# Selective scans: two of sixteen B products made from transposes, and B loads in two buffers instead of three

## The chip, the cores and the metric

The kernel runs on one core of one Trainium2 chip. The metric is the device time of one execution in microseconds (us). Before the change, three runs gave 34,249.87, 34,252.28 and 34,259.34 us; their median, 34,252.28 us, is what a new time is compared with.

## The reference

The reference is a chain of four residual layers on an image of 256 x 256 positions with 128 channels: attention, a state-space layer with selective scans (layer 1), a Fourier layer and a recurrent filter. Ahead of each stands a group norm. Only layer 1 is touched by the change in its arithmetic. Its core:

```python
xs = jnp.concatenate([x_hwwh, jnp.flip(x_hwwh, axis=-1)], axis=1)   # 4 directions
x_dbl = jnp.einsum('bkdl,kcd->bkcl', xs, x_proj_w)
dts, Bs, Cs = jnp.split(x_dbl, [DT_RANK, DT_RANK + D_STATE], axis=2)  # 8, 16, 16 rows
...
def step(h, inp):
    d_t, x_t, B_t, C_t = inp
    dA = jnp.exp(d_t[..., None] * As)
    h = dA * h + (d_t * x_t)[..., None] * B_t[:, :, None, :]
    y = jnp.einsum('bkdn,bkn->bkd', h, C_t)
    return (h, y)
```

There are 4 directions, 256 inner channels, 16 states and 65,536 positions. For each direction, channel, state n and position t, the scan needs a factor exp(delta · A), an input delta · x · B with B the same for all channels, and its result is multiplied by C, also the same for all channels, and summed over the states.

## The kernel before, in words

The scans are `scan_stream` (from line 562). It walks over 512 chunks: four directions (k = 0 and 1 forward, 2 and 3 backward; 1 and 3 over the transposed image), each with 128 chunks of 512 positions. Channels lie on the partitions, in two halves `dh` of 128; positions lie along the row. States are handled in four groups of G = 4. One chunk is therefore NG = 8 steps, numbered `j` (or `s` in the loop): step j has half j % 2 and states of group j // 2. `g` counts steps over all chunks.

A step has these parts. `b_product` (L763) multiplies four rows of B, spread over all partitions (`l1b_bb`, 128 x 4 x 512), by delta · x (one row of 512 per channel) and gives `l1b_db`. Steps 2, 4 and 6 do this on GpSimd with a copy of delta · x in SBUF (`l1b_dus`, made by ScalarE at L752); the others do it on VectorE with delta · x in PSUM (`l1b_mm` for half 0, `l1b_du` for half 1). `scans` makes each pair of states in turn: ScalarE writes exp(delta · A) for two states into a PSUM tile `l1b_da` (L781, two tiles used in turn), sets the column where the second state begins from the state kept from the last chunk (L785), and VectorE runs one scan over both states, 1,024 columns (L796). After the first pair ScalarE keeps the last column of the step before (`keep_state`, L807). `c_product` (L811, GpSimd) multiplies the four scans by C (`l1b_cc`), and `sums` (L830, TensorE) adds the results into PSUM by products with the identity, two steps later. `y_out` (L839, ScalarE) copies the sum, and every second chunk SP stores two chunks of y (L643).

Beside this, the next chunk is prepared: `dt` (L699) and the two identity products `soft_sum` (L725) make delta through softplus (ScalarE L711 to L719), `delta_copy` (L733) keeps it, `delta_x` (L741, VectorE) multiplies it by x, in step 4 for half 0 (into `l1b_mm`) and in step 7 for half 1 (into `l1b_du`). `xproj` (L667) and `xd_copy` (L679) make the 40 rows of delta's input, B and C two chunks ahead; SP writes B and C to DRAM (L681) and reads them back spread over the partitions with `load_b` (L687) and `load_c` (L693), 1 MB each, four of each per chunk.

The order of all this is written out by hand. `tc.manual_schedule()` makes every engine's queue follow the order of the program text, and all DMAs here go through SP's queue in that order too. `b_order` says which products stand ahead of which step (numbers from 8 on belong to the next chunk: product 8 in step 4, product 10 in step 6); `extras` says what stands after the first and the second scan of a step. Product 9 stands in step 7. `load_b` for group g // 2 + 4 and `load_c` for g // 2 + 3 stand at the end of the odd steps, B first. Tiles come from pools with a fixed number of buffers: B and C loads 3 each, products 5, scans 3, C products 3. An instruction that would overwrite a buffer waits until its readers are done, and so does everything behind it in its queue.

## Time and profile before

| what | value |
|---|---|
| runs (median) | 34,252.28 us |
| the profiled execution's own time | 34,251.71 us |
| its span, first to last instruction | 34,249.9 us |
| busy: TensorE / VectorE / ScalarE / GpSimd | 85% / 91% / 66% / 80% |
| scan stage 3,904 to 29,500 us, busy: TensorE / VectorE / ScalarE / GpSimd | 21,390 / 24,930 / 18,017 / 25,264 us |
| DMA share in the scan stage | 0.54 |
| mean granted TensorE clock | 0.918 |

A line of a group names the source line, the engine, the operation, what it writes and reads, the shape and the count; after the bar stand the busy total in us, the mean of one in ns, and the idle time of the engine just before such instructions with what ended most of it. In a timeline the columns are start and length in us, engine, line and operation. SPq is the DMA queue of SP: there the length is the time to issue a transfer, not to move it. A window's line has the busy time of each engine, then the granted clock, the mean share of the 16 DMA engines and the GB/s that they moved.

### The profile page before, as it was taken

What the parts mean: (1) busy time and instruction counts of PE and PEld (TensorE: products, weight loads), DVE (VectorE), ACT (ScalarE), POOL (GpSimd) and SP (SyncE); (2) the same over time, 40 slices, a digit from 0 to 9 for tenths busy, and PEclk for the clock granted to TensorE, in tenths of its full rate; (3) what the DMA queues carried; (4) which work ended last, traced back from release to release, by engine and by line L of the source; (5) the groups of instructions that cost most, each with busy time, mean ns of one, the idle gap of its engine ahead of it and who ended that gap; (6) DMA issues with size and microseconds to landing.
All of it is one profiled execution on the core that took longest, in us unless ns stands there. A gap on an engine that the chain in (4) does not pass through costs nothing. (4 is left out here: it accounts for less than half of the span.)

```text
span 34249.9 us, 256893 instructions
## 1 busy us (share of the span) xinstructions
PE 29062.3 (85%) x72308; PEld 12164.1 (36%) x72308; DVE 31137.1 (91%) x23801; ACT 22770.2 (66%) x46991; POOL 27433.4 (80%) x6996
## 2 busy tenths in 40 slices
PE   7999888888888888888888888888888888899988
PEld 3554333333333333333333333333333333334444
DVE  6668999999999999999999999999999999863699
ACT  3667777777777777777777777777777777532476
POOL 2446899999999999999999999999999999620000
PEclk8999999999999999999999999999999999999888
DMA  3113455555555555555555555555555555674111
GB/s 142 45 45 121 183 191 190 192 189 192 191 190 191 190 192 189 192 191 190 197 201 200 201 203 201 201 201 200 200 201 203 201 201 201 212 236 148 63 34 33
DMA packets 2076530, 5947.88 MB, mean 174 GB/s; under 512 B 115207, under 2 KB 1379608, under 8 KB 1499222
## 3 DMA queue, kind: packets, MB, share of 16 engines
q1 hardware_dynamic: 1939122, 5860.18, 47.3%
q10 hardware_dynamic: 135972, 71.27, 0.7%
q8 instruction: 570, 9.34, 0.1%
q14 instruction: 866, 7.09, 0.1%
HBM read 5238.41 MB, written 692.58 MB: 173 GB/s over the span
## 5 line engine op out<-in xcount | busy, mean ns | idle before, releaser
L796 DVE TENSOR_TENSOR_SCAN l1b_h<-l1b_da,l1b_state,l1b_db 128x1024 f32<-128x1024 f32 x8192 | 18792.7, 2336 | 596.9 <-ACT l1b_db L785 583.3
L811 POOL TENSOR_TENSOR l1b_hc<-l1b_h,l1b_cc 128x2048 f32<-128x2048 f32 x4096 | 18447.2, 4528 | 329.0 <-DVE l1b_h L796 328.0
L830 PE MATMUL l1b_y<-l1b_hc,ident 128*128 128x512 f32 x32768 | 16062.5, 639 | 1117.0 <-POOL l1b_hc L811 1117.0
L781 ACT ACTIVATE l1b_da<-l1b_dl,l_alog 128x512 f32<-128x512 f32 (+1 forms) x16384 | 11297.5, 690 | 3156.6 <-DVE l1b_h L796 2848.7
L830 PEld LDWEIGHTS l1b_y<-l1b_hc,ident 128*128 128x128 f32 x32768 | 6528.7, 205 | 10690.6 <-issue 8162.7
L763 POOL TENSOR_TENSOR l1b_db<-l1b_bb,l1b_dus 128x2048 f32<-128x2048 f32 x1536 | 6967.3, 4536 | 44.5 <-DMA l1b_bb<-l1b_bc 44.5
L763 DVE TENSOR_TENSOR l1b_db<-l1b_bb,l1b_du 128x2048 f32<-128x2048 f32 x2048 | 4657.8, 2274 | 35.2
L785 ACT ACTIVATE l1b_db<-l1b_state,l1b_db,l1b_af 128x1 f32<-128x1 f32 x8192 | 3045.2, 372 | 0.0
L699 PE MATMUL l1b_mm<-l1b_xd,l_dtw 41*128 41x512 f32 x2048 | 1373.1, 755 | 1712.6 <-ACT l1b_dus L752 1706.8
L725 PE MATMUL l1b_mm<-l1b_tail,ident 128*128 128x512 f32 x2048 | 1292.2, 717 | 1380.9 <-ACT l1b_tail L719 1378.5
L807 ACT COPY l1b_state<-l1b_h 128x4 f32<-128x4 f32 x4095 | 789.6, 193 | 2433.8 <-DVE l1b_h L796 2433.7
L327 POOL TENSOR_TENSOR l0b_e<-l0b_e,l0b_den 128x1024 f32<-128x1024 f32 x512 | 969.0, 1893 | 1373.4 <-DVE l0b_den L326 727.3
L725 PE MATMUL l1b_mm<-l1b_relu,ident 128*128 128x512 f32 x2048 | 1308.8, 728 | 0.0
L699 PEld LDWEIGHTS l1b_mm<-l1b_xd,l_dtw 41*128 41x128 f32 x2048 | 337.8, 206 | 2526.4 <-ACT l1b_dus L752 2129.9
L752 ACT COPY l1b_dus<-l1b_mm 128x512 f32<-128x512 f32 x512 | 299.6, 585 | 1388.5 <-DVE l1b_db L763 1388.1
L763 DVE TENSOR_TENSOR l1b_db<-l1b_bb,l1b_mm 128x2048 f32<-128x2048 f32 x512 | 1171.5, 2288 | 18.2 <-ACT l1b_dus L752 0.7
L303 DVE CUSTOM_DVE_ANT_0 l0b_e<-l0b_sc,l0b_bias 128x256 f32<-128x256 f32 x2048 | 745.4, 420 | 414.5 <-PE l0b_sc L292 411.1
L725 PEld LDWEIGHTS l1b_mm<-l1b_tail,ident 128*128 128x128 f32 x2048 | 376.8, 206 | 2051.5 <-ACT l1b_tail L719 1803.9
L318 ACT ACTIVATE l0b_e<-l0b_e,l0b_top 128x256 f32<-128x256 f32 x2048 | 1012.1, 498 | 0.9 <-DVE l0b_top L303 0.9
L667 PE MATMUL l1b_du<-l1b_xc,l_xproj 128*40 128x512 f32 x2048 | 979.8, 601 | 32.2 <-DMA l1b_xc<-l_xc 31.4
L733 ACT COPY l1b_dl<-l1b_mm 128x512 f32<-128x512 f32 x1024 | 587.4, 574 | 524.2 <-DVE l1b_du L741 517.1
L981 POOL TENSOR_TENSOR l1c_y<-l1c_y,l1c_yt 128x512 f32<-128x512 f32 x256 | 396.3, 1570 | 593.1 <-DMA l1c_y<-l_y 528.4
(275 smaller groups left out, 30094.6 us busy)
## 6 DMA issues: line engine op xcount, KB each, us to landing
l1b_bb<-l1b_bc SPq DMA_DIRECT2D x2048, 1024.0 KB
l1b_cc<-l1b_bc SPq DMA_DIRECT2D x2048, 1024.0 KB
l1b_xc<-l_xc SPq DMA_DIRECT2D x128, 1024.0 KB
l_y<-l1b_yo SPq DMA_DIRECT2D x128, 1024.0 KB
l1b_xc<-l_xct SPq DMA_DIRECT2D x256, 512.0 KB
l_y<-l1b_yo SPq DMA_DIRECT2D x256, 512.0 KB
l_xc<-l1a_o SPq DMA_DIRECT2D x64, 1024.0 KB
l_xct<-l1a_ot SPq DMA_DIRECT2D x16, 4096.0 KB
```

Source lines behind the costliest of these rows:

```text
L318: nc.scalar.activation(e[:, i], e[:, i], AF.Exp, scale=-1.0, bias=top[:, i : i + 1], accum_out=den[:, i : i + 1],)
L327: nc.gpsimd.tensor_tensor(e, e, den[:, :, None].to_broadcast([P, 4, S]), ALU.mult)
L667: nc.tensor.matmul(du1[:40], w["xproj"][:, dh, k, :], in_block(blocks[ch][0], ch, dh), start=dh == 0, stop=dh == 1,)
L699: nc.tensor.matmul(mm, w["dt"][:, chunks[ch][0], dh * P : dh * P + P], xds[ch % 3][0:41], start=True, stop=True,)
L725: nc.tensor.matmul(mm, c.ident, part, start=i == 0, stop=i == 1)
L763: eng.tensor_tensor(db, bbs[g // 2], du[:, None, :].to_broadcast([P, G, CH]), ALU.mult)
L781: nc.scalar.activation(da[:, o + lo : o + hi], dl[:, lo:hi], AF.Exp, scale=w["A"][:, k, dh, n : n + 1])
L785: nc.scalar.activation(first, states[k][:, dh, two : two + 1], AF.Identity, scale=af[:, two : two + 1], bias=first,)
L796: nc.vector.tensor_tensor_scan(h_, a_, d_, states[k][:, dh, one : one + 1], ALU.mult, ALU.add)
L807: nc.scalar.copy(states[k][:, dh, n0 : n0 + G], hs[g][:, :, 0 if k >= 2 else CH - 1])
L811: nc.gpsimd.tensor_tensor(hc, hs[g], ccs[g // 2], ALU.mult)
L830: nc.tensor.matmul(ys[j % 2], c.ident, hc[:, i], start=False, stop=j // 2 * G + i == 15)
```

## The change

States 14 and 15 no longer get their B product from a load of B that is spread over the partitions. For them delta · x is turned: TensorE transposes its four blocks of 128 positions (`du_turn`), so that positions lie on the partitions and channels along the row, and ScalarE copies the result to SBUF (`du_keep`). B's 40 rows are turned in the same way (`b_turn`, `b_keep`), which gives one number per position and state. ScalarE then multiplies with B as the per-partition scale (`b_scale`, eight instructions of 128 x 256 per chunk, both halves in one), and TensorE transposes back (`turn_back`, eight transposes in each of steps 6 and 7) into the PSUM tile of the second pair. In these two half steps the exponentials go to a new SBUF tile `l1b_dat`, and the scan reads its factors there and its inputs in PSUM. The addition to the first column is split: the product with the kept state (`from_state`) first, the addition after the turning. A memset clears one column after step 7.

The products of steps 6 and 7 cover two states (`l1b_dbs`, two buffers); the products of four have four buffers instead of five. B loads have two buffers instead of three, the last load of a chunk is half as large, and each now stands at a step of its own: at the end of steps 0 (group 3), 2 and 3 (groups 0 and 1 of the next chunk) and 7 (its group 2). The C loads stand where they stood. Product 10 moves from step 6 to step 7. `dt` for the next chunk moves behind the scans of step 0. There are two tiles `l1b_xd` instead of three. To make room, the group norms' statistics lie in pools of their own that are closed between layers (this part of the diff is left out).

```diff
-    b_order = {0: (3,), 1: (4,), 2: (5,), 3: (6, 7), 4: (8,), 6: (10,)}
+    T, NT = 14, CH // P
+    b_order = {0: (3,), 1: (4,), 2: (5,), 3: (6, 7), 4: (8,)}
+    turned_at = {(0, 1): (0, 1), (1, 0): (2,), (2, 0): (3,), (3, 0): (4,), (4, 1): (5, 6, 7)}
...
         def load_b(m):
             if m < 4 * N:
-                n0 = m % 4 * G
-                bb = bbs[m] = bcp.tile([P, G, CH], F32, name="l1b_bb")
-                nc.sync.dma_start(bb, bcs[m // 4][n0 : n0 + G][None].to_broadcast([P, G, CH]))
+                n0, n = m % 4 * G, min(G, T - m % 4 * G)
+                bb = bbs[m] = bcp.tile([P, G, CH], F32, name="l1b_bb", bufs=2)
+                nc.sync.dma_start(
+                    bb[:, 0:n], bcs[m // 4][n0 : n0 + n][None].to_broadcast([P, n, CH])
+                )
...
-            db = dbs[g] = wk.tile([P, G, CH], F32, name="l1b_db", bufs=5)
+            n = min(G, T - j // 2 * G)
+            name, bufs = ("l1b_db", 4) if n == G else ("l1b_dbs", 2)
+            db = dbs[g] = wk.tile([P, n, CH], F32, name=name, bufs=bufs)
...
+        def b_turn(ch):
+            for b in range(NT):
+                nc.tensor.transpose(
+                    du1[:, bass.ts(b, 40)], xds[ch % 2][0:40, bass.ts(b, P)], c.ident[0:40, 0:40]
+                )
+        def b_keep(ch):
+            bt = bts[ch] = wk.tile([P, NT, 16 - T], F32, name="l1b_bt")
+            nc.scalar.copy(
+                bt, du1[:, 0 : NT * 40].rearrange("p (b n) -> p b n", b=NT)[:, :, 8 + T : 24]
+            )
+        def du1_copy(ch):
+            dls[ch, "du1"] = wk.tile([P, CH], F32, name="l1b_relu", bufs=1)
+            nc.scalar.copy(dls[ch, "du1"], du1)
+        def du_turn(ch, dh):
+            du = dls.pop((ch, "du1")) if dh else dls[ch, "du"]
+            for b in range(NT):
+                nc.tensor.transpose(mm[:, bass.ts(b, P)], du[:, bass.ts(b, P)], c.ident)
+        def du_keep(ch, dh):
+            nc.scalar.copy(duts[ch][:, :, dh], mm.rearrange("p (b c) -> p b c", b=NT))
+        def b_scale(ch, i):
+            n, b = divmod(i, NT)
+            nc.scalar.activation(
+                turned[ch][:, b, n], duts[ch][:, b], AF.Identity, scale=bts[ch][:, b, n : n + 1]
+            )
+        def turn_back(ch, dh, to):
+            for n in range(16 - T):
+                for b in range(NT):
+                    nc.tensor.transpose(to[:, n, bass.ts(b, P)], turned[ch][:, b, n, dh], c.ident)
...
+                if n0 + 2 * i < T:
+                    dbp = db[:, sl]
+                else:
+                    from_state = wk.tile([P, 1], F32, name="l1b_fs")
...
+                    turn_back(ch, dh, das[i])
+                    dbp, da = da, das_t.rearrange("p g t -> p (g t)")
...
                 if s == 7:
-                    extras[0] = [lambda: delta_x(nxt, 1), lambda: b_product(g + 2)]
-                    extras[1] = [lambda: delta_copy(nxt, 1)]
+                    extras[0] = [
+                        lambda: delta_x(nxt, 1),
+                        lambda: b_product(g + 2),
+                        lambda: b_product(g + 3),
+                    ]
+                    extras[1] = [
+                        lambda: delta_copy(nxt, 1),
+                        lambda: du1_copy(nxt),
+                        lambda: du_turn(nxt, 0),
+                    ]
...
                 c_product(g)
+                if s in (0, 2, 3, 7):
+                    load_b(4 * ch + {0: 3, 2: 4, 3: 5, 7: 6}[s])
                 if s % 2 == 1:
-                    load_b(g // 2 + 4)
                     load_c(g // 2 + 3)
```

Also in the diff: `du_keep(nxt, 0)` and `du_turn(nxt, 1)` at the end of step 7, `du_keep(ch, 1)` after the first scan of step 0, `b_turn(nxt)` at the end of step 4 and `b_keep(nxt)` after the first scan of step 5.

## The prediction, made before the changed kernel was run

> **What bounds it now.** I began with the page's totals and its forty slices.
>
> ```profile
> span 34249.9 us, 256893 instructions
> ...
> PE 29062.3 (85%) x72308; PEld 12164.1 (36%) x72308; DVE 31137.1 (91%) x23801; ACT 22770.2 (66%) x46991; POOL 27433.4 (80%) x6996
> ...
> DVE  6668999999999999999999999999999999863699
> ...
> POOL 2446899999999999999999999999999999620000
> ```
>
> VectorE (DVE) and GpSimd (POOL) are both full from slice 4 to slice 34: the scan stage. It runs from about 3,904 to 29,500 us, and the span (34,249.9 us) stands 1.8 us below its own execution (34,251.7) and 2.4 below the median of the runs (34,252.28), so a sum over the stage can be set on either. Next the costliest groups:
>
> ```profile
> L796 DVE TENSOR_TENSOR_SCAN l1b_h<-l1b_da,l1b_state,l1b_db 128x1024 f32<-128x1024 f32 x8192 | 18792.7, 2336 | 596.9 <-ACT l1b_db L785 583.3
> L811 POOL TENSOR_TENSOR l1b_hc<-l1b_h,l1b_cc 128x2048 f32<-128x2048 f32 x4096 | 18447.2, 4528 | 329.0 <-DVE l1b_h L796 328.0
> ...
> L763 POOL TENSOR_TENSOR l1b_db<-l1b_bb,l1b_dus 128x2048 f32<-128x2048 f32 x1536 | 6967.3, 4536 | 44.5 <-DMA l1b_bb<-l1b_bc 44.5
> L763 DVE TENSOR_TENSOR l1b_db<-l1b_bb,l1b_du 128x2048 f32<-128x2048 f32 x2048 | 4657.8, 2274 | 35.2
> ```
>
> Per chunk of 512 positions that is, on VectorE, 16 scans, 5 B products (L763) and 2 multiplications delta·x (L741, 0.674 us each in the groups of 8,000 to 24,000 us); on GpSimd, 8 C products (L811) and 3 B products. In the timeline L741 of one chunk starts at 12,009.48 and of the next at 12,059.42: a chunk lasts 49.94 us, and 512 of them 25,570. On GpSimd 8 × 4.528 + 3 × 4.536 = 49.8 us. On VectorE the records overlap a little (four scans take 9.07 us, five products 2.2 each), 16 × 2.27 + 5 × 2.2 + 1.35 = 48.7; the rest is two gaps of 0.62 and 0.51 us in steps 5 and 6, where the scan waits for ScalarE (ACT). So two engines bound the stage together, and neither queue has room for a new wait.
>
> The next view is the DMA queue's own timeline, since the change alters the B buffers. L693 loads C, L687 loads B, L643 stores y:
>
> ```profile
> 12035.17 0.32 SPq L693 DMA_DIRECT2D l1b_cc<-l1b_bc  x1
> 12035.58 1.28 SPq L643 DMA_DIRECT2D l_y<-l1b_yo  x2
> 12036.96 3.92 SPq L687 DMA_DIRECT2D l1b_bb<-l1b_bc  x1
> ...
> 12085.11 0.32 SPq L693 DMA_DIRECT2D l1b_cc<-l1b_bc  x1
> 12085.52 0.38 SPq L687 DMA_DIRECT2D l1b_bb<-l1b_bc  x1
> ```
>
> SP issues in order. L693 waits for the C product of step 1 to give back its buffer: 12,106 of the 16,000 us from 8,000 to 24,000, the largest of the queue's waits by far. When that product ends is fixed by GpSimd:
>
> ```profile
> 12021.64 4.52 POOL L811 TENSOR_TENSOR l1b_hc<-l1b_h,l1b_cc 128x2048 f32<-128x2048 f32 x1 [0.66 <-DVE l1b_h L796]
> 12026.13 4.52 POOL L763 TENSOR_TENSOR l1b_db<-l1b_bb,l1b_dus 128x2048 f32<-128x2048 f32 x1
> 12030.62 9.00 POOL L811 TENSOR_TENSOR l1b_hc<-l1b_h,l1b_cc 128x2048 f32<-128x2048 f32 x2
> ```
>
> The C product of step 0 starts when its scans end, the B product of state group 2 follows, then the C product of step 1, without a gap: 3 × 4.49 = 13.5 us, to 12,035.1, where SP issues L693. Last, when VectorE begins the first B product of the next chunk, in step 4:
>
> ```profile
> 12040.03 2.29 DVE L763 TENSOR_TENSOR l1b_db<-l1b_bb,l1b_mm 128x2048 f32<-128x2048 f32 x1
> ...
> 12089.97 2.29 DVE L763 TENSOR_TENSOR l1b_db<-l1b_bb,l1b_mm 128x2048 f32<-128x2048 f32 x1
> ```
>
> 12,040.03 − 12,035.17 = 4.86 us after that issue; 89.97 − 85.11 gives 4.86 again. And when the transfers end, from the windows of 1 us (last two columns: share of the DMA engines, GB/s):
>
> ```profile
> 12045.00:12046.00 1.00, 1.00 (x2) 0.34 (x1) 1.00 (x1) 0.97 (x3) 1.00 (x1) 0.50 0.57 238
> 12046.00:12047.00 1.00, 1.00 (x2) 0.34 (x1) 1.00 (x2) 0.36 (x3) 1.00 (x1) 0.50 0.00 0
> ...
> 12086.00:12087.00 1.00, 1.00 (x4) 0.42 (x3) 1.00 (x1) 0.00 (x0) 1.00 (x1) 1.00 1.02 221
> ...
> 12091.00:12092.00 1.00, 0.00 (x0) 0.00 (x0) 1.00 (x1) 0.00 (x0) 1.00 (x1) 1.00 0.53 221
> ```
>
> After the pair of 12,085.11 (C and B, 1 MB each) the engines move data from 12,086.0 to about 12,091.5: 6.4 us from the issue. In the chunk of 12,035.17, with a y store between, they move until 12,045.9: 10.8 us. The other three directions give 6.1, 6.4 and 6.4, and 10.9 with the store (for the last two, whose next B load comes later, 8.3 for C and y plus 2.6 for one load). The B load of these pairs has a buffer to spare now, so nobody waits for it.
>
> **What the Trainium skill says.** "DMA: Bandwidth & Descriptors", section "Anatomy of one DMA — SWDGE (gpsimd) path", gives a fixed part of about 2.0 us per transfer, most of it after the last byte, and says that a semaphore wait is served by the issuing sequencer before dispatch. Its path is GpSimd's and ours SP's; the trace agrees: first packets 0.9 us after the issue, and at the stage's start, where three loads of 1 MB are issued from 3,897.33 (B, C, B), GpSimd waits for the third:
>
> ```profile
> 3897.33 0.34 SPq L687 DMA_DIRECT2D l1b_bb<-l1b_bc  x1
> ...
> 3907.30 4.50 POOL L763 TENSOR_TENSOR l1b_db<-l1b_bb,l1b_dus 128x2048 f32<-128x2048 f32 x1 [44.51 <-DMA l1b_bb<-l1b_bc]
> ```
>
> The windows there add up to 3 MB at about 3,906.1, so the consumer starts some 1.1 us after the last byte, and the third of three transfers is usable 9.97 us after the first issue. Its section "Bandwidth" has 436 GB/s as the divisor; windows with C and B alone show 377 to 467. "TensorE: Matmul & The Clock Gate", section "Part 4: PE-mode transpose", says that a transpose lands in PSUM and needs a copy, at about 275 ns in a kernel; layer 0's transposes show 280 ns each, 137 ns sustained (561.1 us for 4,096). "Perfetto Trace Analysis", section "Optimization Strategy", reads a gap that repeats on the engine that should be full as a possible lack of buffers; today's two gaps are ScalarE's, so the kernel before does not show that.
>
> **The change part by part,** per chunk, against 49.94 us.
>
> Products of states 12–15, now 2 states instead of 4. VectorE: from 0.674 us for 512 columns and 2.288 for 2,048, 1.05 ns a column, so 1,024 columns are cheaper by 1.08 us. GpSimd: 4.536 to about 2.27, its sum to 47.5: no longer a bound. VectorE gains a memset of one column (0.06). Net −1.02 us, −520 us in all if nothing else waits.
>
> ScalarE adds three copies of 128x512 (0.585), eight scalings of 128x256 (the last layer's 128x256 copies take 0.37 to 0.38), two single columns (0.372) and a small copy (0.2): 5.7 us. It is busy 18,016 us of the stage, 35.2 a chunk, so 40.9: not full. It costs only where ScalarE is late already. In step 4 three scalings (0.3 each in spacing) come before the exponentials of step 5, which had 0.46 us to spare; the small copy comes before the softplus in step 5. That moves the gaps from 1.13 to about 1.5: +0.4, bounded by 0 and 1.1 (scalings at the 0.5 of layer 0's 128x256 exponential). The scalings elsewhere and the copies of steps 7 and 0 lie beside VectorE's products (2.2 us each); without that cover they would cost their 0.3 to 0.6 each.
>
> TensorE adds 28 transposes, 3.8 us at 137 ns, to 41.8: under the period. Those that step 6 and 7 wait for may begin when the scan before ends; 8 × 0.137 plus the handover, 1.4 us, lies beside the other half's scan (2.27). The PSUM columns become a scan's second operand in place of its first: I take no cost.
>
> The loads of B. One 1 MB load per chunk shrinks to half. With two buffers, group 0 of the next chunk can be loaded only when the product of step 2 has read its buffer, so its load stands at the end of step 2 in the queue. That puts it behind step 1's C load, which waits for GpSimd until 13.5 us after step 0's scans, and on even chunks behind the y store. Before, it was issued a whole chunk part earlier. VectorE reaches that product 4.86 − 1.08 = 3.8 us after the C load's issue. The load is usable, on odd chunks, 6.4 + 1.1 = 7.5 us after it (9.97 − 2.6 = 7.4 from the start's three loads): a wait of 3.6. On even chunks 10.9 + 1.1 = 12.0: a wait of 8.2. Mean 5.9. GpSimd cannot shorten it: its three products start from VectorE's own scan. Behind the waiting product stand all scans of step 4, and ScalarE's copy L752 waits for it too, so ScalarE gets no lead. GpSimd then waits for the scans. Nothing downstream makes it up. The other B loads are ready: group 1 is issued about 20 us before use, group 3 over 10, group 2 (after the product in step 7) some 13.
>
> Sum: −1.02 + 0.4 + 5.9 = +5.3 us a chunk; 512 × 5.3 = +2,700. The bookkeeping tiles moved to pools of their own run once per layer: a few us at most. 34,252 + 2,700 = **36,950 us**.
>
> **Rivals.** (1) The wait is there but the y store doesn't delay it: all chunks as odd ones, 3.6 us; −1.02 + 0.4 + 3.6 = 3.0, 35,780. For it: the low GB/s at the start of even bursts shows the store moving beside other data; against: bursts end 10.8 us after the issue in the trace, with B's issue last. (2) B arrives in time, as the idle DMA share (54% of the stage busy) suggests; then only ScalarE and TensorE count. If each turned half costs what its transposes and scalings add, 1.1 + 1.0 us, the chunk is longer by 1.1: 34,800. Against: the windows' 6.4 us. (3) The other side: B is usable within 3.8 us of step 1's C load, or is issued ahead of it. Then the products' saving stands, −1.02 + 0.4 = −0.6 a chunk: 33,930. Each us of lateness above that point costs 512 us, so the sign turns at 0.6 us of wait. Against: C alone takes 2.6 us to move after 0.9 of start. That the products are not halved is excluded by the code.
>
> **From these to the numbers.** Main case 0.84, rival 1 0.07, rival 2 0.04, rival 3 0.05. Change that a measurement of this kernel can tell from none: about 0.2%. Slower 0.94, same 0.01, faster 0.05. Range: a mean wait from 4.2 us (completion and store partly hidden) to 6.6, ScalarE 0 to 1.1: 36,050 to 37,600.
>
> **What would show it.** A wait of VectorE's B product from mm on the B load, 512 times, near 3.6 and 8.2 us by turns, about 3,000 us in total; chunk period near 53 and 57.5 by turns; SP's B load 0.4 us after C's on odd chunks; GpSimd with some 8 us idle per chunk; the half products near 1.2 and 2.3 us; scan waits for ScalarE near 750 us. I am wrong if that product never waits for a DMA, or if GpSimd ends step 1's C product earlier after step 0's scans than 13.5 us.

## The result, and the profile after

The changed kernel takes 38,021.2 us (median of four runs, 38,012.47 to 38,029.96) against 34,254.6 us before (median of four runs, the three named above and one more): a ratio of 1.110, 95% interval 1.1086 to 1.1112. The forecast was 36,950 us with a range to 37,600: the right sign, but 1,071 us too little. The profiled execution took 38,012.47 us, its span 38,010.7, so it is 3,760.8 us longer than the span before.

The page's totals and slices of the changed kernel, in the order of the first fence of the prediction:

```profile
span 38010.7 us, 292747 instructions
...
PE 30898.1 (81%) x86644; PEld 13788.8 (36%) x86644; DVE 30827.7 (81%) x24313; ACT 25117.0 (66%) x54159; POOL 26439.6 (70%) x6996
...
DVE  6669888888888888888888888888888888883499
...
POOL 2447788888888888888888888888888888840000
```

VectorE (DVE) and GpSimd (POOL) no longer fill the slices of the scan stage, and VectorE's own work is 309 us less than before (30,827.7 against 31,137.1). The time that was added is in waits. Line numbers have moved: the scan is now L877, the B product L777, the C product L896, the sums L915, the load of B L697, that of C L705, the store of y L653. The page's costliest groups show where the waits are; behind the first bar stand busy time in us and mean length in ns, behind the second the engine's idle time just before, with what ended most of it:

```profile
L877 DVE TENSOR_TENSOR_SCAN l1b_h<-l1b_da,l1b_state,l1b_db 128x1024 f32<-128x1024 f32 x6144 | 14203.3, 2340 | 472.9 <-ACT l1b_state L892 263.5
...
L777 DVE TENSOR_TENSOR l1b_db<-l1b_bb,l1b_mm 128x2048 f32<-128x2048 f32 x512 | 1171.6, 2288 | 2846.0 <-DMA l1b_bb<-l1b_bc 2846.0
L877 DVE TENSOR_TENSOR_SCAN l1b_h<-l1b_dat,l1b_state,l1b_da 128x1024 f32<-128x1024 f32 x1024 | 2400.3, 2344 | 1061.0 <-ACT l1b_da L873 1061.0
...
L877 DVE TENSOR_TENSOR_SCAN l1b_h<-l1b_da,l1b_state,l1b_dbs 128x1024 f32<-128x1024 f32 x1024 | 2393.5, 2337 | 264.0 <-ACT l1b_dbs L869 260.1
```

The second line is the wait that the prediction was about: the product from `mm` waits for its B load, 2,846.0 us, where it stood idle for 18.2 us in all before. The third was not in it: the scan whose second operand TensorE has turned back (`l1b_dat`, the turned scan) waits 1,061.0 us. The other two scan groups wait 472.9 + 264.0 = 736.9 us, where all scans waited 596.9 before. Together 2,827.8 + 1,061.0 + 140.0 − 309.4 = 3,719 us of the 3,761.

The queue of SP and the product that waits, in the timeline of two chunks:

```profile
12010.44 0.32 SPq L705 DMA_DIRECT2D l1b_cc<-l1b_bc  x1
12010.87 6.67 SPq L697 DMA_DIRECT2D l1b_bb<-l1b_bc  x2
...
12065.44 0.32 SPq L705 DMA_DIRECT2D l1b_cc<-l1b_bc  x1
12065.85 1.29 SPq L653 DMA_DIRECT2D l_y<-l1b_yo  x2
12067.31 5.24 SPq L697 DMA_DIRECT2D l1b_bb<-l1b_bc  x2
```

```profile
12017.21 2.29 DVE L777 TENSOR_TENSOR l1b_db<-l1b_bb,l1b_mm 128x2048 f32<-128x2048 f32 x1 [2.89 <-DMA l1b_bb<-l1b_bc]
...
12077.63 2.29 DVE L777 TENSOR_TENSOR l1b_db<-l1b_bb,l1b_mm 128x2048 f32<-128x2048 f32 x1 [8.32 <-DMA l1b_bb<-l1b_bc]
...
12090.60 2.35 DVE L877 TENSOR_TENSOR_SCAN l1b_h<-l1b_da,l1b_state,l1b_dbs 128x1024 f32<-128x1024 f32 x1 [0.51 <-ACT l1b_dbs L869]
12095.91 2.35 DVE L877 TENSOR_TENSOR_SCAN l1b_h<-l1b_dat,l1b_state,l1b_da 128x1024 f32<-128x1024 f32 x1 [2.96 <-ACT l1b_da L873]
```

In the first chunk the B load is issued 0.43 us after the C load and VectorE's product starts 6.77 us after the C load's issue, having waited 2.89. In the second the y store stands between, the product starts 12.19 us after the C load's issue, and the wait is 8.32. Over all 512 chunks of the trace the mean is 3.33 us without a store and 7.79 with one. At the end of the second chunk, in step 6, the turned scan waits another 2.96 us for ScalarE's column L873. What ScalarE waited for is TensorE. Two lines of ScalarE's timeline, then TensorE's between them:

```profile
12079.95 0.59 ACT L764 COPY l1b_dus<-l1b_mm 128x512 f32<-128x512 f32 x1 [11.00 <-DVE l1b_db L777]
...
12095.65 0.24 ACT L873 ACTIVATE l1b_da<-l1b_da,l1b_fs 128x1 f32<-128x1 f32 x1 [3.63 <-PE l1b_da L831]
```

```profile
12080.59 2.07 PE L711 MATMUL l1b_mm<-l1b_xd,l_dtw 41*128 41x512 f32 x2 [9.95 <-ACT l1b_dus L764]
12082.59 6.61 PE L915 MATMUL l1b_y<-l1b_hc,ident 128*128 128x512 f32 x8
12089.13 1.91 PE L677 MATMUL l1b_du<-l1b_xc,l_xproj 128*40 128x512 f32 x4
12090.97 3.70 PE L915 MATMUL l1b_y<-l1b_hc,ident 128*128 128x512 f32 x8
12094.51 1.04 PE L831 MATMUL l1b_da<-ident,l1b_dbt 128*128 128x128 f32 x8
```

ScalarE's copy L764 starts when the late product ends (12,079.92), and dt (L711) waits for that copy. TensorE takes its work in the order of the text, so behind dt stand step 4's sums, the x projection (L677), step 5's sums, and only then the eight transposes that step 6 needs (L831). They begin at 12,094.51. The scan before the turned one began at 12,090.60, so the turned scan was due 2.27 us later, at 12,092.87, and its operand came too late. Note the two rows of sums: eight products take 6.61 us the first time and 3.70 the second. The granted clock, the share of full speed that TensorE is given, differs between them. In windows of 1 us (the third number from the end is the granted clock):

```profile
12073.00:12074.00 1.00, 0.00 (x0) 0.00 (x0) 0.00 (x0) 0.00 (x0) 1.00 (x1) 1.00 1.24 440
...
12075.00:12076.00 1.00, 0.00 (x0) 0.00 (x0) 0.00 (x0) 0.00 (x0) 1.00 (x1) 0.50 1.01 328
...
12087.00:12088.00 1.00, 1.00 (x3) 0.47 (x2) 0.67 (x2) 1.00 (x3) 1.00 (x1) 0.50 0.00 0
...
12089.00:12090.00 1.00, 1.00 (x3) 0.27 (x3) 1.00 (x1) 0.97 (x2) 0.30 (x1) 1.00 0.00 0
```

TensorE stopped at 12,070.6. Some 4 us later, before 12,075, the clock granted drops to 0.50, and it is full again only between 12,088 and 12,089, about 8 us after the work came back at 12,080.6. The Trainium skill, "TensorE: Matmul & The Clock Gate", section "What's actually happening", gives half speed after an idle window of about 3.4 us and full speed after as much sustained work. The half and the idle time agree with these windows; the way back took longer here, and in a chunk further down 1.38 us of idle time just before is enough.

### The profile page after: what moved, and what is told of

Same layout as the page of the kernel before. It is cut to its first block, busy times and chain, and to the rows that moved or that the text cites. A ratio compares the mean times of both kernels' runs of the same rounds, so it can differ in the third digit from the quotient of the medians.

```text
span 38010.7 us, 292747 instructions
## 1 busy us (share of the span) xinstructions
PE 30898.1 (81%) x86644; PEld 13788.8 (36%) x86644; DVE 30827.7 (81%) x24313; ACT 25117.0 (66%) x54159; POOL 26439.6 (70%) x6996
## 4 chain that ended last, share of the span: by engine, by line
DVE 34%; PE 27%; DMA 12%; POOL 9%; issue 5%; ACT 5%; SPq 0%; DVEq 0%; POOLq 0%; ACTq 0%
DVE l1b_h L877 21%; PE l1b_y L915 13%; DMA l1b_bb<-l1b_bc 11%; DVE l1b_db L777 7%; POOL l1b_hc L896 6%; POOL l1b_db L777 3%; PE l1b_mm L711 3%; PE l1b_du L677 2%; DVE l1a_mm L521 1%; PE l2f_fp L1448 1%; PE l1b_da L831 1%; PE l2f_op L1455 1%; ACT l1b_da L863 1%; DVE l1b_du L753 1%; DVE l1b_dbs L777 1%
## 5 line engine op out<-in xcount | busy, mean ns | idle before, releaser
L896 POOL TENSOR_TENSOR l1b_hc<-l1b_h,l1b_cc 128x2048 f32<-128x2048 f32 x4096 | 18535.6, 4533 | 5088.3 <-DVE l1b_h L877 3555.2
L915 PE MATMUL l1b_y<-l1b_hc,ident 128*128 128x512 f32 x32768 | 15926.6, 634 | 17.6 <-POOL l1b_hc L896 9.8
L877 DVE TENSOR_TENSOR_SCAN l1b_h<-l1b_da,l1b_state,l1b_db 128x1024 f32<-128x1024 f32 x6144 | 14203.3, 2340 | 472.9 <-ACT l1b_state L892 263.5
L863 ACT ACTIVATE l1b_da<-l1b_dl,l_alog 128x512 f32<-128x512 f32 (+1 forms) x14336 | 9881.2, 689 | 682.3 <-DVE l1b_h L877 438.9
L915 PEld LDWEIGHTS l1b_y<-l1b_hc,ident 128*128 128x128 f32 x32768 | 6502.7, 204 | 9279.3 <-issue 8327.5
L711 PE MATMUL l1b_mm<-l1b_xd,l_dtw 41*128 41x512 f32 x2048 | 1635.1, 889 | 3920.2 <-ACT l1b_dus L764 3565.8
L777 POOL TENSOR_TENSOR l1b_db<-l1b_bb,l1b_dus 128x2048 f32<-128x2048 f32 x1024 | 4694.8, 4585 | 43.9 <-DMA l1b_bb<-l1b_bc 43.9
L777 DVE TENSOR_TENSOR l1b_db<-l1b_bb,l1b_du 128x2048 f32<-128x2048 f32 x1536 | 3513.7, 2288 | 38.5 <-ACT l1b_db L869 2.0
L777 DVE TENSOR_TENSOR l1b_db<-l1b_bb,l1b_mm 128x2048 f32<-128x2048 f32 x512 | 1171.6, 2288 | 2846.0 <-DMA l1b_bb<-l1b_bc 2846.0
L877 DVE TENSOR_TENSOR_SCAN l1b_h<-l1b_dat,l1b_state,l1b_da 128x1024 f32<-128x1024 f32 x1024 | 2400.3, 2344 | 1061.0 <-ACT l1b_da L873 1061.0
L764 ACT COPY l1b_dus<-l1b_mm 128x512 f32<-128x512 f32 x512 | 300.1, 586 | 4216.0 <-DVE l1b_db L777 4215.6
L877 DVE TENSOR_TENSOR_SCAN l1b_h<-l1b_da,l1b_state,l1b_dbs 128x1024 f32<-128x1024 f32 x1024 | 2393.5, 2337 | 264.0 <-ACT l1b_dbs L869 260.1
L869 ACT ACTIVATE l1b_db<-l1b_state,l1b_db,l1b_af 128x1 f32<-128x1 f32 x6144 | 2283.8, 372 | 0.0
L711 PEld LDWEIGHTS l1b_mm<-l1b_xd,l_dtw 41*128 41x128 f32 x2048 | 404.8, 246 | 4103.7 <-ACT l1b_dus L764 3625.7
L824 ACT ACTIVATE l1b_dbt<-l1b_dut,l1b_bt 128x256 f32<-128x256 f32 x4096 | 1886.0, 496 | 0.0
L873 ACT ACTIVATE l1b_da<-l1b_da,l1b_fs 128x1 f32<-128x1 f32 x1024 | 241.8, 236 | 2305.5 <-PE l1b_da L831 2305.5
L863 ACT ACTIVATE l1b_dat<-l1b_dl,l_alog 128x512 f32<-128x512 f32 (+1 forms) x2048 | 1349.9, 706 | 0.0
L777 POOL TENSOR_TENSOR l1b_dbs<-l1b_bb,l1b_dus 128x1024 f32<-128x1024 f32 x512 | 1208.6, 2361 | 0.0
```

Of the source, the lines that this page charges most:

```text
L711: nc.tensor.matmul(mm, w["dt"][:, chunks[ch][0], dh * P : dh * P + P], xds[ch % 2][0:41], start=True, stop=True,)
L777: eng.tensor_tensor(db, bbs[g // 2][:, 0:n], du[:, None, :].to_broadcast([P, n, CH]), ALU.mult)
L824: nc.scalar.activation(turned[ch][:, b, n], duts[ch][:, b], AF.Identity, scale=bts[ch][:, b, n : n + 1])
L863: nc.scalar.activation(da[:, o + lo : o + hi], dl[:, lo:hi], AF.Exp, scale=w["A"][:, k, dh, n : n + 1])
L869: nc.scalar.activation(first, state, AF.Identity, scale=af[:, two : two + 1], bias=first)
L877: nc.vector.tensor_tensor_scan(h_, a_, d_, states[k][:, dh, one : one + 1], ALU.mult, ALU.add)
```

## Experiments

Kernels for which no ratio is given were timed once. Those timed several times spread by 45 us at most, and the differences that single runs are used for are 490 us and more, with one exception that is named.

Two theories on the load wait were open: that the order of SP's queue makes it (mine), or that the load is just too slow for two buffers. And for the 1,061 us: that TensorE's queue makes them, or that the turning itself (transposes and ScalarE's scalings) takes too long for one scan's length.

**The B load issued ahead.** The load of the next chunk's group 0 is issued right after the product that frees its buffer, ahead of the y store and of step 1's C load, which moves to the end of step 2.

```diff
@@ in the loop over steps
+                if s == 2:
+                    load_b(4 * ch + 4)
                 extras = [[], []]
...
-                if s in (0, 2, 3, 7):
-                    load_b(4 * ch + {0: 3, 2: 4, 3: 5, 7: 6}[s])
-                if s % 2 == 1:
+                if s in (0, 3, 7):
+                    load_b(4 * ch + {0: 3, 3: 5, 7: 6}[s])
+                if s == 2:
+                    load_c(4 * ch + 3)
+                if s % 2 == 1 and s > 1:
```

> The changed kernel with one thing moved in SP's queue: group 0's B load for the next chunk is issued right behind the product of step 2 that frees its buffer, ahead of the y store and of step 1's C load (which goes behind it, to the end of step 2). My theory: the 2,846 us of VectorE's waiting for that load vanish, and with them most of the 1,061 us in which the turned scans wait, since those come from TensorE's queue being held behind the same product: 34,000 to 34,350 us. Rival (the turned half steps are late by themselves, because their transposes stand behind two groups of sums in TensorE's queue): only the DMA wait goes, the 1,061 us stay: about 35,150 us.

Measured: 34,196.6 us, ratio to before 0.9982, interval 0.9975 to 0.9988. VectorE's groups of this kernel:

```profile
L877 DVE TENSOR_TENSOR_SCAN l1b_h<-l1b_dat,l1b_state,l1b_da 128x1024 f32<-128x1024 f32 x1024 | 2390.5, 2334 | 134.8 <-ACT l1b_da L873 134.7
...
L777 DVE TENSOR_TENSOR l1b_db<-l1b_bb,l1b_mm 128x2048 f32<-128x2048 f32 x512 | 1170.9, 2287 | 18.3 <-ACT l1b_dus L764 0.7
```

No load is waited for any more, and the turned scans' wait falls from 1,061.0 to 134.8 us with it. So two buffers are enough: the 3,767 us that the change lost come back with the places of two loads in the queue, and 58 more. The turning is as it was, so the turning by itself is not what took 1,061 us: its lateness followed from the load's.

**The loads alone.** The kernel before, with two B buffers and the changed kernel's load places, and no turning.

```diff
-                bb = bbs[m] = bcp.tile([P, G, CH], F32, name="l1b_bb")
+                bb = bbs[m] = bcp.tile([P, G, CH], F32, name="l1b_bb", bufs=2)
...
+                if s in (0, 2, 3, 7):
+                    load_b(4 * ch + {0: 3, 2: 4, 3: 5, 7: 6}[s])
                 if s % 2 == 1:
-                    load_b(g // 2 + 4)
                     load_c(g // 2 + 3)
```

> The kernel before, without any turning, with two B buffers instead of three and the B loads at the new places in the queue (all loads 1 MB). My theory: VectorE reaches the product 1.1 us later than in the changed kernel, so it waits 6.8 - 4.9 = 1.9 us on odd and 12.2 - 4.9 = 7.3 us on even chunks, 4.6 on the mean, 2,360 us: 36,500 to 36,750 us. Rival (it is the turning's load on the engines that makes the loads late): 34,250 us.

Measured: 36,627.2 us, 2,373 more than before. VectorE's group:

```profile
L763 DVE TENSOR_TENSOR l1b_db<-l1b_bb,l1b_mm 128x2048 f32<-128x2048 f32 x512 | 1171.5, 2288 | 2395.0 <-DMA l1b_bb<-l1b_bc 2394.4 <-ACT l1b_dus L752 0.7
```

The wait for the load is the whole loss, and no scan waits longer than before (597.6 us). With the turning VectorE comes to the product 1.08 us earlier in each chunk, 553 us in all, and the wait grows by nearly as much: from 2,394 to 2,846 us in the changed kernel, and to between 2,852 and 2,900 in three runs below where it stands late as well. Most of what the halved products save is waited away at once. The Trainium skill, "Perfetto Trace Analysis", section "Optimization Strategy", says that a gap that repeats on the engine that should be full can mean a lack of buffers. Here it is that (the third buffer is what the kernel before has more), and a lack that the issue order can make good.

**The B load ahead of the store only.** B stands behind the C load as in the change, but ahead of the y store.

```diff
+                if s == 2:
+                    load_b(4 * ch + 4)
                 extras = [[], []]
...
-                if s in (0, 2, 3, 7):
-                    load_b(4 * ch + {0: 3, 2: 4, 3: 5, 7: 6}[s])
+                if s in (0, 3, 7):
+                    load_b(4 * ch + {0: 3, 3: 5, 7: 6}[s])
```

> The changed kernel with group 0's B load issued behind step 1's C load as in the change, but ahead of the y store. My theory: even chunks wait like odd ones, about 3.1 us each, 1,600 us in all instead of 2,846; the turned scans' wait stays about 1,000: 36,700 to 36,850 us. Rival (the store moves beside the loads and does not delay them; the alternation has another cause): 38,000 us.

Measured: 37,402.4 us, between the two expectations and so a miss: the load wait is 2,144.0 us, and 1,600 was expected; the turned scans wait 1,148.2 us. Two chunks of VectorE's timeline, the first without and the second with a store:

```profile
12001.69 2.29 DVE L777 TENSOR_TENSOR l1b_db<-l1b_bb,l1b_mm 128x2048 f32<-128x2048 f32 x1 [3.41 <-DMA l1b_bb<-l1b_bc]
...
12058.18 2.29 DVE L777 TENSOR_TENSOR l1b_db<-l1b_bb,l1b_mm 128x2048 f32<-128x2048 f32 x1 [4.67 <-DMA l1b_bb<-l1b_bc]
```

With the store behind it the load is still later than without one: over all 512 chunks the mean wait is 4.92 against 3.46 us, where 7.79 against 3.33 was seen with the store ahead. So most of the store's price is its place ahead of the load. A part of some 1.5 us is left when it is issued 0.4 us behind, while the load still moves. (The 3.41 us above and the 2.89 of the changed kernel are one chunk each; without a store most chunks of both lie between 2.9 and 4 us.)

**dt behind the sums.** The changed kernel, with step 4's dt behind that step's sums in TensorE's queue; the loads stay late.

```diff
                 if s == 4:
                     b_turn(nxt)
-                    dt(nxt, 1)
...
                     sums(g - 2)
+                if s == 4:
+                    dt(nxt, 1)
```

> The changed kernel with one thing moved in TensorE's queue: the delta product of step 4 (which waits for ScalarE's copy L764, and that for the B product that waits for the DMA) stands behind step 4's sums instead of ahead of them. The B load stays late. My theory: the DMA wait stays near 2,850 us, and the turned scans' wait falls from 1,061 us to under 350, because the sums run while VectorE is stalled: 37,200 to 37,400 us. Rival (turned half steps late by themselves): nothing changes, 38,000 us.

Measured: 37,529.6 us, 492 less than the changed kernel, but short of the expectation (37,200 to 37,400); the turned scans wait 521.7 us, where under 350 was expected, the load 2,896.7. Half of the 1,061 us came from dt's place. TensorE's timeline shows the other half:

```profile
12067.96 2.07 PE L711 MATMUL l1b_mm<-l1b_xd,l_dtw 41*128 41x512 f32 x2 [6.20 <-ACT l1b_dus L764]
12072.53 3.63 PE L677 MATMUL l1b_du<-l1b_xc,l_xproj 128*40 128x512 f32 x4 [2.50 <-ACT l1b_bt L794]
```

The x projection now stands ahead, waiting for ScalarE's small copy of the turned B (L794), which is behind the stall too; and it runs at half clock, 3.63 us instead of 1.91.

**The x projection behind as well.** On top of the last one the projection goes behind step 6's transposes.

```diff
                 if s == 6:
-                    extras[1] = [lambda: xd_copy(ch + 2)]
+                    extras[1] = [lambda: xproj(ch + 2), lambda: xd_copy(ch + 2)]
...
-                if s == 5:
-                    xproj(ch + 2)
```

> On top of the run with dt behind step 4's sums (37,529.6 us; turned scans' wait 521.7 us, load wait 2,896.7): the x projection, which stood in TensorE's queue ahead of step 5's sums and of the transposes of step 6, goes behind those transposes. My theory, the turned scans wait because of what stands in TensorE's queue ahead of their transposes: their wait falls to 135 to 250 us, as with the B load ahead, the load wait stays near 2,900, the time is 37,150 to 37,270. Rival, the rest of the wait comes from ScalarE, which runs late by itself after the stall: the wait stays at 450 to 550 us and the time at 37,500.

Measured: 37,540.4 us, the rival's time, but not for the rival's reason. (That it is 11 us more than in the run before is the exception: no more than the spread.) VectorE's groups:

```profile
L877 DVE TENSOR_TENSOR_SCAN l1b_h<-l1b_da,l1b_state,l1b_dbs 128x1024 f32<-128x1024 f32 x1024 | 2405.8, 2349 | 852.6 <-ACT l1b_dbs L869 846.3 <-ACT l1b_fs L852 6.3
L877 DVE TENSOR_TENSOR_SCAN l1b_h<-l1b_dat,l1b_state,l1b_da 128x1024 f32<-128x1024 f32 x1024 | 2387.1, 2331 | 1.6 <-ACT l1b_da L873 1.4
```

The turned scans wait 1.6 us: what held them stood in TensorE's queue. But the next scan (`l1b_dbs`) waits 852.6 us instead of 264.1. ScalarE now meets the projection's copy L689 before that scan's exponentials, and L689 waits 0.99 us for the projection at 12,080.77. The wait went on by one scan.

**The order mended on both engines.** Turning of B, its small copy and the projection are moved up to step 3 and the head of step 4, and dt stays behind step 4's sums, so that only dt and step 5's sums stand between the late product and the transposes, and ScalarE waits for nothing late. The loads are still those of the change.

```diff
                 if s == 4:
-                    extras[0] = [lambda: du_copy(nxt)]
+                    extras[0] = [lambda: b_keep(nxt), lambda: xproj(ch + 2), lambda: du_copy(nxt)]
...
-                if s == 5:
-                    extras[0].insert(0, lambda: b_keep(nxt))
...
+                if s == 3:
+                    b_turn(nxt)
                 scans(g, extras)
...
-                if s == 4:
-                    b_turn(nxt)
-                    dt(nxt, 1)
-                if s == 5:
-                    xproj(ch + 2)
...
+                if s == 4:
+                    dt(nxt, 1)
```

> The changed kernel with its loads as they are, but nothing ahead of step 6's transposes in TensorE's queue except sums: dt behind step 4's sums, and the turning of B, its copy and the x projection in step 3 and at the head of step 4, so that neither TensorE nor ScalarE waits for them late in the chunk. With dt and the projection behind, 37,540 us was measured, because the wait went on to the next scan (852.6 us instead of 264). My theory, that was ScalarE waiting for the late projection: here the turned scans wait below 150 us and the next ones about 264, so 37,529.6 - 400 = 37,050 to 37,200 us, the load wait near 2,900. Rival, a stall of 2.9 to 8.3 us is made up by no order, and the wait only changes its place: 37,450 to 37,600.

Measured: 36,958.8 us, somewhat below the expectation. VectorE's groups:

```profile
L877 DVE TENSOR_TENSOR_SCAN l1b_h<-l1b_dat,l1b_state,l1b_da 128x1024 f32<-128x1024 f32 x1024 | 2387.4, 2331 | 6.8 <-ACT l1b_da L873 4.9
L777 DVE TENSOR_TENSOR l1b_db<-l1b_bb,l1b_mm 128x2048 f32<-128x2048 f32 x512 | 1171.1, 2287 | 2900.8 <-DMA l1b_bb<-l1b_bc 2900.2 <-ACT l1b_dus L764 0.7
```

The turned scans wait 6.8 us, the others 465.7 + 263.7, and the load wait is what it was. 38,021.2 − 36,958.8 = 1,062 us: the turned scans' wait, taken away without touching the loads. What is left comes within 9 us of the prediction's 36,950. That closeness is luck in part: the load wait is some 140 us less than predicted, and VectorE's work saves 357 us instead of 522.

**A version that beats both?** With the B load ahead, VectorE still had three gaps of 0.53, 0.32 and 0.52 us in steps 5 and 6, all behind ScalarE. I first moved three scalings from behind step 4's second scan to its first half, where ScalarE was waiting.

```diff
-    turned_at = {(0, 1): (0, 1), (1, 0): (2,), (2, 0): (3,), (3, 0): (4,), (4, 1): (5, 6, 7)}
+    turned_at = {(0, 1): (0, 1), (1, 0): (2,), (2, 0): (3,), (3, 0): (4,)}
...
-                    extras[0] = [lambda: du_copy(nxt)]
+                    extras[0] = [lambda i=i: b_scale(ch, i) for i in (5, 6, 7)]
+                    extras[0] += [lambda: du_copy(nxt)]
```

> On top of the kernel with the B load ahead (34,196.6 us): the three scalings of turned columns that ScalarE makes after step 4's second scan are made at the head of step 4's first half, where ScalarE stands about 2.7 us waiting for the product that its copy of mm waits for. VectorE's gaps there were 0.53 us (step 5, behind ScalarE's copy of the states), 0.32 and 0.52 us a chunk. My theory, ScalarE's order makes these gaps: the first of them goes, 0.5 us x 512 = 250 us, so 33,900 to 34,000 us. Rival, the scalings don't matter, the softplus parts behind the scan do alone: within 60 us of 34,200.

Measured: 34,333.6 us, ratio 1.0024 (1.0015 to 1.0034): worse than with the scalings late, by 137 us, so both numbers were wrong. The first gap went, but the second grew to 0.69 us and the turned scans' wait from 134.8 to 366.6 us. These waits come in the chunks in which TensorE's first sums behind dt are slower than 3.75 us (3.70 is their time at full clock): 310 of 511 here, 115 in the run with the B load ahead. Why they are more isn't shown.

Then the softplus of the next chunk's second half was spread over steps 4 to 6, one part per scan, on top of that (`soft_part` 0 to 3 are Abs, Relu, Exp and Ln of `soft_abs` and `soft_exp`).

```diff
-                    extras[0] += [lambda: du_copy(nxt)]
+                    extras[0] += [lambda: du_copy(nxt), lambda: dt(nxt, 1)]
+                    extras[1] = [lambda: soft_part(nxt, 0)]
                 if s == 5:
-                    extras = [[lambda: soft_abs(nxt)], [lambda: soft_exp(nxt)]]
+                    extras = [[lambda: soft_part(nxt, 1)], [lambda: soft_part(nxt, 2)]]
...
                 if s == 6:
-                    extras[1] = [lambda: xd_copy(ch + 2)]
+                    extras = [[lambda: soft_part(nxt, 3)], [lambda: xd_copy(ch + 2)]]
...
                     b_turn(nxt)
-                    dt(nxt, 1)
```

> On top of the run with the scalings early, the softplus of the next chunk's second half is spread: its dt product and Abs in step 4, Relu and Exp in step 5, Ln in the first half and the copy of x_dbl in the second half of step 6, where they stood in pairs. My theory, that VectorE's remaining 1.4 us of gaps a chunk are ScalarE's pairs standing ahead of the next scan's exponentials: the gaps fall to about 0.3 us a chunk, 33,600 to 33,700 us, below the kernel before by 1.7%. Rival, GpSimd's 47.3 us and VectorE's 48.2 us a chunk and their buffers hold the end: no better than 34,000.

Measured: 34,369.7 us, ratio 1.0034 (1.0021 to 1.0046), far above the expectation and in the rival's range. ScalarE's gaps did fall, from 655 to 140 us without the turned scans, but those wait 950.6. TensorE's timeline of one chunk (the transposes are L848 here, the sums L932, the projection L677):

```profile
12029.57 1.12 PE L711 MATMUL l1b_mm<-l1b_xd,l_dtw 41*128 41x512 f32 x2 [3.09 <-ACT l1b_dus L781]
...
12030.84 5.40 PE L932 MATMUL l1b_y<-l1b_hc,ident 128*128 128x512 f32 x8
12036.17 1.91 PE L677 MATMUL l1b_du<-l1b_xc,l_xproj 128*40 128x512 f32 x4
12038.01 3.70 PE L932 MATMUL l1b_y<-l1b_hc,ident 128*128 128x512 f32 x8
12041.55 1.04 PE L848 MATMUL l1b_da<-ident,l1b_dbt 128*128 128x128 f32 x8
```

It is the same queue again, with no late load at all: dt begins at 12,029.57 behind ScalarE's copy, the sums take 5.40 us after 3.09 us of idle time (the granted clock is 0.50 from 12,031 to 12,034), the projection and the second sums follow, and the transposes begin at 12,041.55. The scan before the turned one began at 12,038.23 and lasted to 12,040.56. So the last kernel takes the turning of B, its copy and the projection out from between, as above.

```diff
+                if s == 3:
+                    b_turn(nxt)
                 scans(g, extras)
...
                 if s == 4:
-                    extras[0] = [lambda i=i: b_scale(ch, i) for i in (5, 6, 7)] + [lambda: du_copy(nxt), lambda: dt(nxt, 1)]
+                    extras[0] = [lambda: b_keep(nxt), lambda: xproj(ch + 2)]
+                    extras[0] += [lambda i=i: b_scale(ch, i) for i in (5, 6, 7)] + [lambda: du_copy(nxt), lambda: dt(nxt, 1)]
...
-                if s == 5:
-                    extras[0].insert(0, lambda: b_keep(nxt))
...
-                if s == 4:
-                    b_turn(nxt)
-                if s == 5:
-                    xproj(ch + 2)
```

> On top of the spread kernel (34,369.7 us, where the turned scan of step 6 waits 950.6 us and every other scan 140): the turning of B, the small copy of it and the x projection are taken out of TensorE's queue between step 4's sums and the transposes of step 6, and put in step 3 and at the head of step 4. In the spread kernel these transposes began 1.0 us after the scan before them could have been followed. My theory, what stands in TensorE's queue ahead of the transposes makes that wait: some 2.3 us come out from ahead of them, the wait falls below 200 us and the time to 33,500 to 33,700, under both kernels. Rival, the sums ahead of them wait for GpSimd's products, which can't be earlier: the wait stays above 700 us and the time above 34,100.

Measured: 33,588.7 us, ratio 0.9806 (0.9790 to 0.9823), as expected. VectorE's groups:

```profile
L894 DVE TENSOR_TENSOR_SCAN l1b_h<-l1b_da,l1b_state,l1b_db 128x1024 f32<-128x1024 f32 x6144 | 14161.8, 2338 | 255.3 <-ACT l1b_db L886 186.7 <-ACT l1b_state L909 1.8 <-POOL l1b_hc L913 0.5
...
L894 DVE TENSOR_TENSOR_SCAN l1b_h<-l1b_dat,l1b_state,l1b_da 128x1024 f32<-128x1024 f32 x1024 | 2399.8, 2344 | 39.9 <-ACT l1b_da L890 0.8
L894 DVE TENSOR_TENSOR_SCAN l1b_h<-l1b_da,l1b_state,l1b_dbs 128x1024 f32<-128x1024 f32 x1024 | 2380.7, 2325 | 1.3 <-POOL l1b_hc L913 1.2
```

All scans together wait 297 us, half of the 597 of the kernel before. The rivals of the last two runs are refuted: neither full engines nor late sums kept the time above 34,000.

**The same spreading without the turning.** The kernel before, with the softplus spread in the same way and nothing else changed.

```diff
                 if s == 4:
-                    extras[0] = [lambda: du_copy(nxt)]
+                    extras[0] = [lambda: du_copy(nxt), lambda: dt(nxt, 1)]
+                    extras[1] = [lambda: soft_part(nxt, 0)]
                 if s == 5:
-                    extras = [[lambda: soft_abs(nxt)], [lambda: soft_exp(nxt)]]
+                    extras = [[lambda: soft_part(nxt, 1)], [lambda: soft_part(nxt, 2)]]
                 if s == 6:
-                    extras[1] = [lambda: xd_copy(ch + 2)]
+                    extras = [[lambda: soft_part(nxt, 3)], [lambda: xd_copy(ch + 2)]]
...
-                if s == 4:
-                    dt(nxt, 1)
```

> The kernel before with the same spreading of the softplus parts, without the turning and with three B buffers as it has. VectorE has 1.13 us of gaps a chunk there and GpSimd is busy 49.8 of 49.94 us. My theory, GpSimd is as full as VectorE before, so ScalarE's order alone gives at most 0.1 us a chunk: 34,150 to 34,260 us. Rival, the gaps behind ScalarE are the bound and GpSimd follows: 1 us a chunk less, 33,700 us.

Measured: 33,932.0 us, ratio 0.9907 (0.9893 to 0.9920): far below my expectation, and above the rival's. GpSimd's groups from 8,000 to 24,000 us:

```profile
L828 POOL TENSOR_TENSOR l1b_hc<-l1b_h,l1b_cc 128x2048 f32<-128x2048 f32 x2597 | 12035.1, 4889 | 2.3 <-DVE l1b_h L813 2.3
L780 POOL TENSOR_TENSOR l1b_db<-l1b_bb,l1b_dus 128x2048 f32<-128x2048 f32 x973 | 4765.2, 4897 | 0.0
```

GpSimd is now without a gap, 3,570 instructions in 16,000 us: 4.482 us each, 49.30 a chunk of 11. Its records overlap when they follow each other, so their length (4.89 here, 4.53 in the kernel before) is not what one costs. Before, it took 49.94 us a chunk and so had 0.64 us to give, which is the 0.66 us gap that its own timeline shows in each chunk. That much was gained (320 us / 512 = 0.63). From here on GpSimd is the bound: with no gap left in it, order alone has nothing more to give. The turning takes half a product from it, and the fastest kernel is a further 343 us lower (33,932.0 to 33,588.7). I take these as the turning's worth; the two kernels differ in the order of loads and of the x projection as well, which no run separates.

## Why the prediction was right and wrong

| step, us over 512 chunks | predicted | measured |
|---|---|---|
| idle time ahead of the product from `mm` (load wait) | +3,020 | +2,828 |
| work of VectorE | −522 | −309 |
| scans behind ScalarE, without the turned ones | +205 | +140 |
| TensorE's turning | 0 | +1,061 |
| sum | +2,700 | +3,719 (span: +3,761) |

**The load wait: right.** It comes in every chunk, on the mean 3.33 us without a store and 7.79 with one, where 3.6 and 8.2 were worked out. The cause is shown: the load alone makes 2,394 us of wait in the kernel before, and its place makes them go.

**The work: half right.** The products fell as costed: the half ones last 1,196 ns on VectorE and 2,361 on GpSimd, and VectorE's products are 532 us less in all, the memset apart. But VectorE's busy time as a whole fell by 309 us only. A part of this may be overlap: records of scans are 2.34 us long and follow each other every 2.27, and where a scan starts after a gap the overlap of 0.07 is missing. More gaps are not the whole reason, though. In the fastest kernel above the scans wait half as long as in the kernel before, and VectorE's work is still only 400 us less (30,737.1), not 522. What makes up the rest stays open.

**ScalarE: right.** 0.27 us a chunk, between the bounds of 0 and 1.1, and in the place that was named: the first gap of step 5 goes when the three scalings of step 4 are moved. The scalings take 496 ns each instead of the 0.37 to 0.38 us of the copies.

**TensorE: the step that failed.** "Those that step 6 and 7 wait for may begin when the scan before ends; 8 × 0.137 plus the handover, 1.4 us, lies beside the other half's scan (2.27). [...] I take no cost." The length was right: eight transposes take 1.04 us. What was wrong is when they may begin: not when the scan before ends, but when TensorE is through with what stands ahead of them in its queue, and that runs at half clock. The prediction considers what the transposes read and overwrite, and not this queue. Shown in its place are 1,061.0 us of waiting, 2.07 us a chunk. Both the queue and the half clock were to be seen in the trace of the kernel before, in TensorE's timeline after the product of 12,040.03:

```profile
12042.99 1.12 PE L699 MATMUL l1b_mm<-l1b_xd,l_dtw 41*128 41x512 f32 x2 [3.18 <-ACT l1b_dus L752]
12044.04 5.40 PE L830 MATMUL l1b_y<-l1b_hc,ident 128*128 128x512 f32 x8
12049.37 1.91 PE L667 MATMUL l1b_du<-l1b_xc,l_xproj 128*40 128x512 f32 x4
12051.21 3.70 PE L830 MATMUL l1b_y<-l1b_hc,ident 128*128 128x512 f32 x8
12054.75 1.02 PE L725 MATMUL l1b_mm<-l1b_tail,ident 128*128 128x512 f32 x2
```

dt waits for the copy behind that product, the sums behind it take 5.40 us after an idle 3.18, and TensorE is through with step 5's sums at 12,054.75. In 485 of the 511 chunks that can be read, these sums take longer than 3.75 us; it cost nothing, because no scan waited for them. After them the transposes were to go. The scan that they feed is due at 12,040.03 + 2.2 + 5 × 2.27 + 1.13 = 12,054.7 us, and with their 1.04 us they end more than 1 us after that.

How much of the wait is the half clock? In the changed kernel's chunk above, dt to the last transpose takes 14.96 us; at full clock dt and the first sums would take 1.12 + 3.70 instead of 2.07 + 6.61 us, 3.9 us less, more than the 2.96 us of that wait. The run with the B load ahead settles it, since it has the same order, and dt starts 2.96 us after the product in it as in the changed kernel. Two chunks of it, first TensorE, then the turned scans:

```profile
18311.87 1.61 PE L711 MATMUL l1b_mm<-l1b_xd,l_dtw 41*128 41x512 f32 x2 [1.38 <-ACT l1b_dus L764]
18313.40 6.56 PE L915 MATMUL l1b_y<-l1b_hc,ident 128*128 128x512 f32 x8
...
18364.00 1.12 PE L711 MATMUL l1b_mm<-l1b_xd,l_dtw 41*128 41x512 f32 x2 [1.43 <-ACT l1b_dus L764]
18365.05 3.70 PE L915 MATMUL l1b_y<-l1b_hc,ident 128*128 128x512 f32 x8
```

```profile
18326.68 2.35 DVE L877 TENSOR_TENSOR_SCAN l1b_h<-l1b_dat,l1b_state,l1b_da 128x1024 f32<-128x1024 f32 x1 [2.44 <-ACT l1b_da L873]
...
18376.28 2.32 DVE L877 TENSOR_TENSOR_SCAN l1b_h<-l1b_dat,l1b_state,l1b_da 128x1024 f32<-128x1024 f32 x1
```

With the first sums at half clock (0.50 from 18,313 to 18,319) the turned scan waits 2.44 us, with full clock not at all. In 511 chunks of that run, 396 have these sums in 3.70 us and no wait; the other 115 have slower sums and 132 us of the 134.8. In the changed kernel the sums are slower than 3.75 us in all 511 chunks. So it takes both, and both are shown: the same order at full clock makes no wait (these 396 chunks), and with the order mended there is none either, though its trace has sums of 5.40 us after a stall as well. The late load has its part in that it leaves TensorE idle in every chunk.

**What bound the kernel before: partly wrong.** I called VectorE and GpSimd bound together and left no room in GpSimd, from 49.8 us of records in 49.94. The kernel before with its softplus spread shows that ScalarE's order was worth 0.63 us a chunk, and that GpSimd's real time is 49.3. This moved no number of the forecast, in which GpSimd is relieved anyway.

**The range.** Its ends don't follow from the terms that it names. With the mean wait at 4.2 us and ScalarE at 0 the sum is 35,880 us, with 6.6 and 1.1 it is 37,670; 36,050 and 37,600 were stated. Neither reaches 38,021, because no term for TensorE was in it.

**Rivals.** The first (the store doesn't delay) is refuted by 2.89 against 8.32 us. The second has the turned halves costing something beside VectorE, which they do, but with its B load in time, which it isn't. The third, faster at 33,930 once the load is issued ahead, was tried: 34,196.6. The sign is right, and it misses by 267 us: the turned scans wait 135 us, which was put at nothing, and VectorE's work falls by 348 us instead of 522. (The other scans' 138 us were allowed for, with 205.)

**What should be seen** was seen: the wait on the product in every chunk; SP's B load 0.43 us behind C's; GpSimd's C products waiting 5,088 us, 9.3 a chunk more than before (329 us; 8 were forecast). Eight chunks from 12,017 us on last 54.4 to 56.1 and 59.2 to 60.4 us by turns instead of 53 and 57.5; the turned scan's 1.5 to 3 us are most of that.

## What to carry to other kernels

Giving up a buffer moves the earliest moment of a load, and with it its place in the queue; price the wait from what stands ahead there, then see whether a place further up is free. For every new instruction that another engine waits for, read the timeline of its own engine at the point where it goes in: what stands ahead, what that waits for, and, on TensorE, whether it runs at half clock there. A stall on one engine can come back a second time on another, in the same chunk, as here.

## What the runs showed of the hardware

- TensorE at half clock lasts well beyond the idle time ahead of it: granted 0.50 until about 8 us after work resumed, eight sums of 128x512 in 6.61 us instead of 3.60 to 3.70.
- The idle time just before doesn't decide it alone: after 1.38 us of it the eight sums took 6.56 us in one chunk, after 1.43 us 3.70 in the next.
- The mean granted clock is no measure of the time: 0.895 in the changed kernel, but 0.883 in the faster one with the loads alone (36,627.2 us); 0.918 in the kernel before, 0.947 in the fastest one.
- A store of 1 MB, in one or two transfers, issued 0.4 us behind a load of 1 MB still makes that load some 1.5 us later (4.92 against 3.46 us of wait on the mean).
- Back-to-back GpSimd products of 128x2048 have records of 4.53 us, in one run 4.89, but follow each other every 4.48 to 4.49 in both; on an engine without gaps the count tells the time, not the sum of the records.
